# Two runs of packed 32x32 products in place of one, in a linear-attention kernel on one Trainium2 core

## The chip, the cores and the metric

The kernel runs on one core of a Trainium2 chip. The core has a matrix engine (TensorE, PE in the profile, with its weight loads shown apart as PEld), a vector engine (VectorE, DVE), a scalar engine (ScalarE, ACT), a general engine (GpSimd, POOL) and an engine that here only issues transfers (SyncE, SP). Matrix products go into PSUM, of which the kernel uses eight banks of 128 x 512 fp32 values; everything else lies in SBUF, and the inputs and the output in HBM. Each engine works off its own queue of instructions in order, and engines wait for each other by semaphores. The metric is the device time of one execution in microseconds; lower is better.

## The reference

Sixteen sequences of 256 tokens with 128 features go through twelve layers of attention without a softmax, then a layer norm, a gated feed-forward and a second layer norm. The core of a layer:

```python
for i in range(12):
    qkv = x @ Wqkv[i].T + bqkv[i]
    q, k, v = split(qkv)                # 16 heads of 8 features
    att = einsum('bhqd,bhkd->bhqk', q, k) * scale
    y   = einsum('bhqk,bhkd->bhqd', att, v)
    x   = y @ Wproj[i].T + bproj[i] + x
x = layernorm(x0 + x)
h = silu(x @ wg.T) * (x @ wu.T)
x = layernorm(x + h @ wd.T)
```

Without a softmax the order of the products is free: y = q (k^T v) per head, and k^T v is only 8 x 8 per head. The kernel goes further and never moves the tokens through the layers at all.

## The kernel before

Within a sequence a layer multiplies every token by one and the same matrix, which depends on the sequence, so the kernel carries one 128 x 128 matrix and one offset column per sequence (`tst`, 128 x 130 with two spare columns). Sixteen sequences are taken as eight *pairs* of two batches (`PB = 2`), and four pairs make a *set* (`G = 4`, `NO = 2`): two sets for each of the twelve layers, 24 in all. fp32 matrices that go through PE are split into a rounded high part and a low part (`thl`, `whl`, `yhl`), so that a product is three fast ones.

Per layer and pair, `products` (L420) makes K and V (`mm_kv`, L436 to L438, six full-size products of 256 columns), Q (`mm_q`, L444 to L446, three of 260 columns) and g0 times V (`mm_gv`, L457, two fp32 products of 128 columns, which the profile shows as four passes). Copies out of PSUM (L440, L449, L459) go through the helper `copy`, so the profile shows them at L205 (ACT) or L207 (DVE).

Per layer and set, `heads` (L480) does what is packed. `mm_m` (L493) makes the heads' small matrices in products of 128 rows by 32 columns (L501, and the offsets' L382 before them). DVE adds an offset (L511) and masks (L513), which gives `gm`: for each pair and batch a 128 x 32 strip that holds four 32 x 32 blocks. Then `mm_y` (L515) multiplies each 32 x 32 block of `gm` with the matching 32 rows of Q (130 columns) on PE's 32 x 32 tiles:

```python
for b in range(PB):
    for r, p in enumerate(pairs):
        for g in range(G):
            nc.tensor.matmul(bank(pys[r])[group(g + r), ...], gm[group(g), r * PB + b, :], qss[p][group(g), b, :], ...)
```

The loops over r and g address each of the 16 tiles once; the second batch addresses the same 16 again. A set has 2 x 4 x 4 = 32 such products in four PSUM banks (`pys`), and as each is fp32 it is issued as two passes with a weight load each: 64 rows at L519.

`projection` (L523) then casts y out of PSUM (L531, by ACT or DVE), takes the low part (L532, DVE), multiplies by the output weights (`mm_w`, L536 to L538; two more at L540 and L541 in the last layer), and adds to `tst` (L543). In the layers but the last, a cast by ACT (L545) and a subtraction by POOL (L546) make the next layer's `thl`. After the last layer each pair goes through the feed-forward (`ffn`, L575).

No instruction order is written out. Every step is an `Op` of a `Plan` with a cost per engine that may do it, what it reads and writes, and a priority. `Plan.run` (L118) is a list scheduler that runs when the program is built: it keeps a time for each engine, computes for each ready step when it could start, takes the earliest start and among those that could start by then the lowest priority, and emits it. The time at which a step may follow another is the other's end plus a constant: 300 for PE behind ACT, DVE or POOL, 30 for PE behind PE (L137). PSUM banks, raw weights and split weights are slots that the same planner hands out. Its costs only set the order and the choice of engine; on the chip semaphores decide. The step of y costs 1200 (L520), one product on rounded fp32 `0.447 n + 5`, that of `mm_m` 890 and 140 for each set of offsets that rides along.

In the built program the order on PE around a set is, in the layers from 2 on: three products of the last Q, twelve of K and V of the other set's first two pairs, the 64 rows of y, twelve of the other two pairs' K and V, one pair's L457, twelve of the projection, three pairs' L457, nine of Q, then the next set's `mm_m`.

Of the kernel before, what the change touches and what calls it, by code (L numbers as in the profile page):

```python
# [25 lines left out]
PB = 2  # L26
NP = B // PB
W = C + 2
# [8 lines left out]
G = 4  # L37
# [13 lines left out]
LSTEP = 0.05  # L51
WLEAD = 0.6
TAILW = 0.0001
AHEAD = 0.16
SPARE = 500

# [17 lines left out]
PE, ACT, DVE, POOL, SP = "pe", "act", "dve", "pool", "sp"  # L74
AFTER = {PE: 270, ACT: 160, DVE: 200, POOL: 180, SP: 3000}
TO_PE = 300


class Val:


    def __init__(self, kind=None):
        self.kind, self.slot = kind, None
        self.writers, self.readers, self.ops, self.left = [], [], [], 0


class Op:
    def __init__(self, n, costs, emit, prio):
        self.n, self.costs, self.emit, self.prio = n, costs, emit, prio
        self.end = self.engine = None  # L90
        self.deps, self.users, self.vals = set(), [], []


class Plan:
    def __init__(self, slots):
        self.slots, self.ops = slots, []

    def op(self, costs, emit, reads=(), writes=(), prio=0.0):

        o = Op(len(self.ops), costs, emit, prio)  # L100
        for v in reads:
            o.deps.update(v.writers)
        for v in writes:
            o.deps.update(v.writers, v.readers)
            v.writers, v.readers = [o], []
        for v in reads:
            if v not in writes:
                v.readers.append(o)
        o.vals = list(dict.fromkeys([*reads, *writes]))
        for v in o.vals:  # L110
            if v.kind:
                v.left += 1
                v.ops.append(o)
        for d in o.deps:
            d.users.append(o)
        self.ops.append(o)

    def run(self):  # L118
        free = dict.fromkeys(AFTER, 0.0)
        free.update({SP: 800.0, DVE: 4000.0, ACT: 3200.0, POOL: 4900.0})  # L120
        slots = {k: [(0.0, i) for i in range(n)] for k, n in self.slots.items()}
        left = {o: len(o.deps) for o in self.ops}
        for o in reversed(self.ops):
            o.tail = min(o.costs.values()) + 300 + max((u.tail for u in o.users), default=0)
        ready = [o for o in self.ops if not left[o]]
        takes = lambda o: [v for v in o.vals if v.kind and v.slot is None]
        while ready:
            found = []
            for o in ready:
                if any(not slots[v.kind] for v in takes(o)):  # L130
                    continue
                held = max((min(slots[v.kind])[0] for v in takes(o)), default=0.0)
                best, least = None, None
                for e, c in o.costs.items():
                    t = max(free[e], held)
                    for d in o.deps:
                        wait = TO_PE if e == PE and d.engine in (ACT, DVE, POOL) else 30 if d.engine == e == PE else AFTER[d.engine]  # L137
                        t = max(t, d.end + wait)
                    rank = t + c + (SPARE if e == DVE and o.prio > L - 1.6 else 0)
                    if best is None or rank < least:  # L140
                        best, least = (t, t + c, e), rank
                found.append((best, o))
            assert found, "no slot is free"
            first = min(b[0] for b, _ in found)
            (_, end, e), o = min(((b, o) for b, o in found if b[0] <= first), key=lambda x: (x[1].prio - TAILW * x[1].tail, -x[1].tail, x[1].n))
            o.engine, o.end = e, end
            free[e] = end
            ready.remove(o)
            for v in takes(o):
                s = min(slots[v.kind])  # L150
                slots[v.kind].remove(s)
                v.slot = s[1]
            o.emit(e)
            for v in o.vals:
                if v.kind:
                    v.left -= 1
                    if not v.left:
                        slots[v.kind].append((max(x.end for x in v.ops) + 200, v.slot))
            for u in o.users:
                left[u] -= 1  # L160
                if not left[u]:
                    ready.append(u)
        assert all(o.end is not None for o in self.ops)
        self.span = max(free.values())
# [14 lines left out]
def dve(n, fast=False):  # L179
    return 69 + n / (1.92 if fast else 0.96)  # L180


def pool(n):
    return 147 + 2.1 * n
# [7 lines left out]
def linear_attention_ffn_kernel(ctx: ExitStack, tc: tile.TileContext, x, xt, wall, wq0, bias, wg, wu, wd, out):  # L192
    nc = tc.nc
# [5 lines left out]
    plan = Plan({"bank": 8, "raw": RAW, "weights": WSLOTS, "turned": WSLOTS})  # L199
    banks = [ps.tile([128, 512], F32, name=f"bank{i}") for i in range(8)]  # L200
    bank = lambda v: banks[v.slot]
# [10 lines left out]
    def mul(e, dst, a, b):  # L212
        (nc.vector if e == DVE else nc.gpsimd).tensor_tensor(dst, a, b, ALU.mult)  # L213
# [55 lines left out]
    vq, vgv = [Val() for _ in range(NP)], [Val() for _ in range(NP)]  # L269
# [50 lines left out]
    qss = [t[:, : PB * W].rearrange("p (a b) -> p a b", b=W) for t in qgvs]  # L320
# [3 lines left out]
    vt, vc, vhi, vlo, vm, vg0, vkv, vyh, vyl, vqo, vw = (named() for _ in range(11))  # L324
# [48 lines left out]
    def offset_products(l, o):  # L373

        raw, pc = wts[l][0], Val("bank")
        c = tst[:, o * OB : (o + 1) * OB, C]

        def mm():
            for s in range(1 if l else 0, 3):
                for g in range(G):  # L380
                    cols = slice(32 * g, 32 * g + 32)
                    nc.tensor.matmul(bank(pc)[cols, s * OB : (s + 1) * OB], wraw[raw.slot][:, s * C : (s + 1) * C][:, cols], c, start=True, stop=True)  # L382
        return [raw, *vc[o * G : (o + 1) * G]], pc, mm
# [34 lines left out]
    vgm = sets()  # L418
# [55 lines left out]
    def first_offsets(o, prio):  # L474
        def fill(e):
            for p in range(o * G, (o + 1) * G):
                nc.gpsimd.tensor_copy(qss[p][:, :, C], qc[:, p * PB : (p + 1) * PB])
        plan.op({POOL: 600}, fill, [vqc[o]], vqo[o * G : (o + 1) * G], prio)

    def heads(l, o, prio, riders):  # L480

        raw = wts[l][0]
        pairs = range(o * G, (o + 1) * G)
        gm = gms[o]
        pm, pys = Val("bank"), [Val("bank") for _ in pairs]
        group = lambda g: slice(32 * (g % G), 32 * (g % G) + 32)
        src = [raw] if l == 0 else [vkv[p] for p in pairs]

        more = [(*r, *offset_products(*r)) for r in riders]

        def mm_m(e):  # L493
            for _, _, _, _, mm in more:
                mm()
            for p in pairs:
                for b in range(PB):
                    n = (p - o * G) * PB + b
                    tk = wraw[raw.slot][:, C : 2 * C] if l == 0 else kvs[p][:, b, 0, :]
                    for g in range(G):  # L500
                        nc.tensor.matmul(bank(pm)[group(g), n * 32 : n * 32 + 32], tk[:, group(g)], gvs[p][:, b, group(g)], start=True, stop=True)  # L501
        reads = [v for _, _, rs, _, _ in more for v in rs]
        if l == 0 and o == 1:

            reads += vw[:G]
        plan.op({PE: 890 + 140 * len(more)}, mm_m, [*(vgv[p] for p in pairs), *src, *reads], [pm, *(m[3] for m in more)], prio)
        for lo, oo, _, pc, _ in more:
            offsets(lo, oo, prio + (OFFSET if lo else 0), pc)
            if lo == 0:
                first_offsets(o, prio)  # L510
        plan.op({DVE: dve(OB * 32)}, lambda e: nc.vector.tensor_tensor(  # L511
            gm, bank(pm)[:, : OB * 32].rearrange("p (b j) -> p b j", j=32), kvo[:, o * OB : (o + 1) * OB], ALU.add), [pm, vkvo[o]], [vgm[o]], prio)
        plan.op({DVE: dve(OB * 32), POOL: pool(OB * 32)}, lambda e: mul(e, gm, gm, mask32.unsqueeze(1).to_broadcast([128, OB, 32])), [], [vgm[o]], prio)  # L513

        def mm_y(e):  # L515
            for b in range(PB):
                for r, p in enumerate(pairs):
                    for g in range(G):
                        nc.tensor.matmul(bank(pys[r])[group(g + r), b * W : (b + 1) * W], gm[group(g), r * PB + b, :], qss[p][group(g), b, :], start=True, stop=True)  # L519
        plan.op({PE: 1200}, mm_y, [vgm[o], *(vq[p] for p in pairs), *(vqo[p] for p in pairs)], pys, prio)  # L520
        return pys

    def projection(l, p, py, prio):  # L523
# [234 lines left out]
    for p in range(NP):  # L758
        ffn(p, L + FOFF + FSTEP * p - (AHEAD if p == NP - 1 else 0))
    plan.run()  # L760
# [31 lines left out]
```

## Time and profile before

| | |
|---|---|
| time, median of 3 runs | 306.25 us (306.08 to 306.49) |
| the profiled execution | 306.32 us, of which its span 304.6 us |
| instructions | 12894 |
| PE busy, products | 295.0 us, 5382 |
| PE rows at L519 (y, 32x32) | 1536, 25.8 us busy |
| PE rows at L501 (128x32) | 1536, 18.6 us busy |
| mean clock that TensorE was granted | 0.996 |

The profile is of one execution. Its span runs from the first to the last instruction; the device time has some 1.7 us around it. Products on PE are pipelined: a row's length is its latency, and rows overlap, so a start-to-start distance is what a product costs in a dense stream. In the page's slices each digit is the busy share of a fortieth of the span (7.6 us) in tenths. A line of the waits names the waiting group, what it waited for, the sum in us, how often, and the longest.

### The profile page before, as it was taken

How to read it: one execution, taken by the hardware profiler on the slowest of the kernel's cores; microseconds unless marked ns; L12 is line 12 of the kernel's file. 1: busy time of each engine (PE TensorE's matmuls, PEld its weight loads, DVE VectorE, ACT ScalarE, POOL GpSimd, SP SyncE). 2: the span in 40 equal slices, each digit the busy share in tenths (PEclk: the TensorE clock that was granted, in tenths of full speed). 3: DMA queues.
4: the chain of work that ended last, by engine and by line, in shares of the span. 5: the costliest groups of instructions: out<-in, count | busy, mean ns of one | idle time of the engine just before them, and what ended most of it. 6: DMA issues, size and time to landing. Idle time of an engine off the chain costs nothing.

```text
span 304.6 us, 12894 instructions
## 1 busy us (share of the span) xinstructions
PE 295.0 (97%) x5382; PEld 270.8 (89%) x5382; DVE 226.6 (74%) x685; ACT 221.2 (73%) x564; POOL 140.7 (46%) x232
## 2 busy tenths in 40 slices
PE   8999999999999999999999999999999999989981
PEld 8989999999999999999999999999999898868870
DVE  4796877777677676876768777786545689999993
ACT  3556877767777768777686666876887567888875
POOL 6246352334531445215442254324433458767783
PEclk9999999999999999999999999999999999999998
DMA  7634213112031120311302102130000000000224
GB/s 209 156 101 126 71 39 88 38 46 81 3 88 37 40 89 3 88 40 31 95 2 56 37 21 61 33 80 4 2 2 3 4 1 2 0 0 2 70 69 139
DMA packets 22490, 15.66 MB, mean 51 GB/s; under 512 B 1952, under 2 KB 19872, under 8 KB 22432
## 3 DMA queue, kind: packets, MB, share of 16 engines
q1 hardware_dynamic: 21872, 14.62, 17.2%
q8 instruction: 42, 0.69, 1.0%
q10 hardware_dynamic: 560, 0.22, 0.3%
q14 instruction: 16, 0.13, 0.1%
HBM read 8.02 MB, written 2.10 MB: 33 GB/s over the span
## 4 chain that ended last, share of the span: by engine, by line
PE 81%; DVE 11%; ACT 3%; issue 3%; POOL 0%; POOLq 0%; DVEq 0%
PE bank L457 14%; PE bank L436 8%; PE bank L519 8%; PE bank L438 7%; PE bank L437 7%; PE bank L501 5%; PE bank L444 5%; PE bank L538 4%; PE bank L537 4%; PE bank L536 4%; PE bank L445 3%; PE bank L446 3%; PE bank L338 3%; DVE st L599 2%; DVE xt L704 2%
## 5 line engine op out<-in xcount | busy, mean ns | idle before, releaser
L210 POOL TENSOR_TENSOR thl<-tst,thl 128x260 fp32r<-128x260 f32 x88 | 64.9, 769 | 123.2 <-ACT thl L205 123.2
L205 ACT COPY qgv<-bank 128x256 f32<-128x256 f32 x170 | 60.8, 377 | 20.7 <-PE bank L446 13.4
L205 ACT COPY kv<-bank 128x512 f32<-128x512 f32 (+1 forms) x93 | 53.4, 577 | 18.8 <-PE bank L438 13.6
L436 PE MATMUL bank<-whl,thl 128*128 128x256 f32 x176 | 51.8, 294 | 0.0
L438 PE MATMUL bank<-whl,thl 128*128 128x256 f32 x176 | 49.7, 282 | 0.0
L437 PE MATMUL bank<-whl,thl 128*128 128x256 f32 x176 | 49.4, 281 | 0.0
L457 PE MATMUL bank<-kv,g 128*128 128x128 f32 x352 | 46.0, 275 | 0.0
L543 DVE TENSOR_TENSOR tst<-bank,tst 128x260 f32<-128x260 f32 x96 | 36.9, 425 | 11.2 <-PE bank L538 9.0
L205 ACT CAST thl<-tst 128x260 fp32r<-128x260 f32 x88 | 33.1, 410 | 14.5 <-DVE tst L543 14.4
L457 PEld LDWEIGHTS bank<-kv,g 128*128 128x128 f32 x352 | 42.7, 191 | 0.4 <-issue 0.4
L450 DVE TENSOR_SCALAR qgv<-bank,bcol 128x2 f32<-128x2 f32 x88 | 19.3, 221 | 27.8 <-ACT qgv L205 23.4
L532 DVE TENSOR_TENSOR yhl<-bank,yhl 128x260 fp32r<-128x260 f32 x96 | 34.5, 421 | 3.0 <-ACT yhl L205 3.0
L436 PEld LDWEIGHTS bank<-whl,thl 128*128 128x128 f32 x176 | 33.1, 188 | 4.1 <-issue 3.8
L438 PEld LDWEIGHTS bank<-whl,thl 128*128 128x128 f32 x176 | 33.1, 188 | 0.2 <-POOL thl L210 0.2
L437 PEld LDWEIGHTS bank<-whl,thl 128*128 128x128 f32 x176 | 33.2, 189 | 0.0
L444 PE MATMUL bank<-thl,whl 128*128 128x260 f32 x88 | 28.9, 328 | 0.0
L519 PE MATMUL bank<-qgv,gm 32*32 32x130 f32 x1536 | 25.8, 280 | 0.2 <-DVE gm L213 0.2
L205 ACT CAST yhl<-bank 128x260 fp32r<-128x260 f32 (+1 forms) x62 | 22.4, 412 | 4.7 <-PE bank L519 4.5
L207 DVE CAST yhl<-bank 128x260 fp32r<-128x260 f32 x42 | 16.1, 424 | 12.9 <-PE bank L519 12.9
L445 PE MATMUL bank<-thl,whl 128*128 128x260 f32 x88 | 24.8, 282 | 0.0
L446 PE MATMUL bank<-thl,whl 128*128 128x260 f32 x88 | 24.7, 281 | 0.0
L519 PEld LDWEIGHTS bank<-qgv,gm 32*32 32x32 f32 x1536 | 17.2, 103 | 5.5 <-ACT kv L205 0.3
(155 smaller groups left out, 704.3 us busy)
## 6 DMA issues: line engine op xcount, KB each, us to landing
wraw<-wall SPq DMA_DIRECT2D x12, 256.0 KB, 2.9
wpt<-whl SPq DMA_DIRECT2D x24, 96.0 KB, 2.2
qgv<-x SPq DMA_DIRECT2D x8, 256.0 KB, 5.2
xt<-xt SPq DMA_DIRECT2D x8, 256.0 KB, 3.2
out<-kv SPq DMA_DIRECT2D x7, 256.0 KB, 2.3
wpt<-whl SPq DMA_DIRECT2D x24, 64.0 KB, 2.6
wpt<-whl SPq DMA_DIRECT2D x24, 32.0 KB, 1.9
wraw<-wg SPq DMA_DIRECT2D x1, 192.0 KB, 3.6
```

The costliest lines, as they stand in the source:

```text
L205: nc.scalar.copy(dst, src)
L210: (nc.vector if e == DVE else nc.gpsimd).tensor_tensor(dst, a, b, ALU.subtract)
L436: nc.tensor.matmul(o, hi[:, b, 0:C], hl(0, 1, 2), start=True, stop=False)
L437: nc.tensor.matmul(o, hi[:, b, 0:C], hl(1, 1, 2), start=False, stop=False)
L438: nc.tensor.matmul(o, lo[:, b, 0:C], hl(0, 1, 2), start=False, stop=True)
L444: nc.tensor.matmul(o, hl(0, 0), flat(hi), start=True, stop=False)
L445: nc.tensor.matmul(o, hl(0, 0), flat(lo), start=False, stop=False)
L446: nc.tensor.matmul(o, hl(1, 0), flat(hi), start=False, stop=True)
L457: nc.tensor.matmul(bank(pgv)[:, b * C : (b + 1) * C], g0[p][:, b, :], tv(b), start=True, stop=True)
L519: nc.tensor.matmul(bank(pys[r])[group(g + r), b * W : (b + 1) * W], gm[group(g), r * PB + b, :], qss[p][group(g), b, :], start=True, stop= ...
L532: plan.op({DVE: dve(PB * W)}, lambda e: nc.vector.tensor_tensor(yl, bank(py)[:, : PB * W], yh.bitcast(F32), ALU.subtract), [py, vyh[p]], [ ...
L543: plan.op({DVE: dve(PB * W)}, lambda e: nc.vector.tensor_tensor(ts, bank(pw)[:, : PB * W], ts, ALU.add), [pw], [vt[p], vc[p]], prio)
```

## The change

The step of y becomes two steps for each set, one per batch (`range(1)`, `range(1, PB)`), each with 16 products and a planner cost of 520. Both write the same four banks, so the planner runs the second behind the first, and the second's distance to the end of the first is now `APART = 300` in place of 30: a step of PE that can start within that time goes first. Readers of y depend on the second step alone. The first set of layer 0 keeps one step at cost 1200.

```diff
+APART = 300
 class Op:
-    def __init__(self, n, costs, emit, prio):
-        self.n, self.costs, self.emit, self.prio = n, costs, emit, prio
+    def __init__(self, n, costs, emit, prio, apart):
+        self.n, self.costs, self.emit, self.prio, self.apart = n, costs, emit, prio, apart
...
-    def op(self, costs, emit, reads=(), writes=(), prio=0.0):
-        o = Op(len(self.ops), costs, emit, prio)
+    def op(self, costs, emit, reads=(), writes=(), prio=0.0, apart=30):
+        o = Op(len(self.ops), costs, emit, prio, apart)
...
-                        wait = TO_PE if e == PE and d.engine in (ACT, DVE, POOL) else 30 if d.engine == e == PE else AFTER[d.engine]
+                        wait = TO_PE if e == PE and d.engine in (ACT, DVE, POOL) else o.apart if d.engine == e == PE else AFTER[d.engine]
...
-        def mm_y(e):
-            for b in range(PB):
-                for r, p in enumerate(pairs):
-                    for g in range(G):
-                        nc.tensor.matmul(bank(pys[r])[group(g + r), b * W : (b + 1) * W], gm[group(g), r * PB + b, :], qss[p][group(g), b, :], start=True, stop=True)
-        plan.op({PE: 1200}, mm_y, [vgm[o], *(vq[p] for p in pairs), *(vqo[p] for p in pairs)], pys, prio)
+        for run in ([range(1), range(1, PB)] if l + o else [range(PB)]):
+            def mm_y(e, run=run):
+                for b in run:
+                    for r, p in enumerate(pairs):
+                        for g in range(G):
+                            nc.tensor.matmul(bank(pys[r])[group(g + r), b * W : (b + 1) * W], gm[group(g), r * PB + b, :], qss[p][group(g), b, :], start=True, stop=True)
+            plan.op({PE: 520 if l + o else 1200}, mm_y, [vgm[o], *(vq[p] for p in pairs), *(vqo[p] for p in pairs)], pys, prio, APART if run[0] else 30)
```

Lines of the changed kernel are two higher than before from L100 on, and four higher behind `mm_y`.

## The prediction

> **What bounds the kernel now.** I read the page's head and its slices first, then what TensorE (PE) waited for, then the timeline of one layer, and last the final stretch.
>
> ```profile
> span 304.6 us, 12894 instructions
> PE 295.0 (97%) x5382; PEld 270.8 (89%) x5382; DVE 226.6 (74%) x685; ACT 221.2 (73%) x564; POOL 140.7 (46%) x232
> ...
> PE   8999999999999999999999999999999999989981
> ...
> DVE  4796877777677676876768777786545689999993
> ```
>
> PE is full in every slice up to the 35th; DVE only fills up in the last seven or so. A busy PE alone proves little, so the waits decide:
>
> ```profile
> PE bank L225 <- DVE qgv L223: 1.0, 1, 1.0
> PE bank L713 <- DVE xt L704: 1.0, 1, 1.0
> ...
> PE bank L519 <- DVE gm L213: 0.2, 1, 0.2
> ```
>
> Over the twelve layers PE waits for nobody but twice for 0.2 us (L519 and L538); the waits of a microsecond are at the start and in the feed-forward. So in the layers the time is the sum of PE's start-to-start distances, and whatever the change adds or saves there moves the end one for one. One run of y (L519) among its neighbours, PE alone:
>
> ```profile
> 151.64 0.28 PE L437 MATMUL bank<-whl,thl 128*128 128x256 f32 x1
> 151.76 0.28 PE L438 MATMUL bank<-whl,thl 128*128 128x256 f32 x1
> 151.97 1.07 PE L519 MATMUL bank<-qgv,gm 32*32 32x130 f32 x64
> 152.98 0.39 PE L436 MATMUL bank<-whl,thl 128*128 128x256 f32 x1
> 153.20 0.28 PE L437 MATMUL bank<-whl,thl 128*128 128x256 f32 x1
> 153.32 0.28 PE L438 MATMUL bank<-whl,thl 128*128 128x256 f32 x1
> ```
>
> First column: start. Full-size products follow each other every 0.118 us (151.64, 151.76; 153.20, 153.32). Into the run the step is 0.21, the run holds PE from 151.97 to 152.98, and the first full-size product behind it is followed only after 0.22. The 64 rows are 32 products, each issued as two passes. Cutting the timeline just before and just after the middle separates the two batches:
>
> ```profile
> 151.97 0.50 PE L519 MATMUL bank<-qgv,gm 32*32 32x130 f32 x32
> ...
> 152.29 0.75 PE L519 MATMUL bank<-qgv,gm 32*32 32x130 f32 x32
> ```
>
> The batches are unequal: 0.50 us for the first 32, 0.75 for the second, which begins 0.32 us into the run. The weight loads say why (PEld and its count, in three stretches of the same run):
>
> ```profile
> 151.90:152.22 0.32, 0.25 (x32) 0.24 (x33) 1.00 0.00 0
> 152.22:152.39 0.17, 0.17 (x33) 0.09 (x1) 1.00 0.00 0
> 152.39:152.79 0.40, 0.40 (x45) 0.37 (x31) 1.00 0.00 0
> ```
>
> Thirty-three loads go out at once, then one in 0.17 us, then 31: the second batch uses the same 16 tiles and cannot load until the first has let go of them. So one long run has a stall inside it as well as the switches at its ends.
>
> **The change, priced.** To the nanosecond, from the single records behind these rows (22 of the 24 runs have the same inner times): last full-size start to first y start 209; first y start to the start of the 32nd 235; to the 33rd 320, 34th 431, 64th 805; from the last y start to the next full-size start 199; from there to the one after 223. Without a run in between, two steps of 118 would stand in these places.
>
> (a) Removed: one run. It costs 209 + 805 + 199 + 223 - 236 = 1200 ns.
>
> (b) Added: two runs of 32. No trace shows such a run alone, but every piece has a row. Entry 209, 32 starts in 235, exit 199 + 223, less 236: 630 ns. Two are 1260, so a set loses 60 ns. Put the other way: the second batch costs 805 - 235 = 570 inside the long run, with its stall (235 to 431) and its slower pace (374 ns from the 34th to the 64th start); by itself it runs like the first, but pays 91 to enter (209 - 118), 199 to leave and 105 (223 - 118) for the first weights behind it: 630.
>
> Is the exit really 199 after a shorter run? The head's other packed products (L501, 128x32) say what it consists of:
>
> ```profile
> 159.06 0.75 PE L501 MATMUL bank<-qgv,kv 128*32 128x32 f32 x64
> 159.74 0.39 PE L444 MATMUL bank<-thl,whl 128*128 128x260 f32 x1
> 159.97 0.28 PE L445 MATMUL bank<-thl,whl 128*128 128x260 f32 x1
> ```
>
> There the last start to the next full-size start is 126 ns, and then 224 again. Their moving side is 32 columns, that of y 130; at the 111 ns per 128-column pass of L457 the difference is 85 ns, and 199 - 126 = 73. So the exit is the last product's streaming plus 86 to 98 ns (199 less 113, 126 less 28) that do not depend on what ran before. I take 199.
>
> Bounds. Low: if a short run leaves as L501 does (126), it costs 557, and a set gains 1200 - 1114 = 86 ns. High: the slowest first batch in the trace (the run at 26.5 us, second set of layer 0) takes 332 for its 32 starts; if every second run did, a set would lose 60 + 97 = 157 ns. The value taken is the plain one, +60, as 22 of the 24 first batches took 235.
>
> The pace inside a short run is the other thing to doubt. In the trace the first 16 starts take 100 ns, 6.7 each, and the second pass begins at 135. [...]
>
> (c) Number: 24 sets, the first of layer 0 excepted: 23 x 60 = 1.4 us. The order in which the changed program issues its instructions has 46 runs of half the length, and never two in a row: between them stand one pair's six K and V products (L436-438) from layer 2 on, two to six other full-size products in layers 0 and 1 and in the last set.
>
> (d) Moved. Around the run, before: q3 kv12 [y] kv12 gv2 w12 gv6; after: q3 kv12 [y] kv6 [y] kv6 gv4 w12 gv4 (w: the projection, L536-538; counts of instructions or products). The same products, and the same number of changes between fp32 and rounded fp32. Two waits come nearer. The casts of y (L531) start only when the second run is over, and w now has kv6 and gv4 ahead of it instead of kv12 and gv2. From the second run's first start: the next full-size start at 235 + 199 = 434, the sixth of kv 223 + 4 x 118 later at 1129, gv from 1247 with eight passes of 111 to 2024, w at some 2.05 us, and its third product, which needs the low part (L532), 324 ns behind at 2.38. On ACT the order is now the copy of the third pair's K and V (0.58) and then the cast of y (0.41): that copy can start when its products end, 0.07 us after the second run's start, so the cast ends at 1.1 and L532 on DVE (0.42) at 1.55. About 0.8 us to spare; cost nothing, cover named. Without the cover each 0.1 us late would cost 2.2 us over the sets. The wait for gm is as before, since M, q3 and kv12 stand in the same order before the first run. The DMA queue's order is unchanged; POOL's changes only in small copies and offsets and in the feed-forward.
>
> (e) The tail. From 254 us DVE sets the pace:
>
> ```profile
> 254.00:270.00 16.00, 14.98 (x87) 12.29 (x86) 15.79 (x30) 11.96 (x24) 11.86 (x10) 1.00 0.00 1
> 270.00:290.00 20.00, 20.00 (x99) 16.37 (x98) 19.37 (x40) 18.34 (x39) 15.49 (x16) 1.00 0.10 27
> ```
>
> (third bracketed column DVE: 35.2 of 36 us; fourth ACT: 30.3). The planner deals the tail's work out anew: three scalings L622 leave DVE and become twelve L627 on ACT; two casts to hh, one subtraction and one copy to yhl go the other way. With the rows' median lengths, DVE's work behind the last mask product falls from 67.9 to 67.3 us, ACT's behind the last cast to thl rises from 72.1 to 74.5. If DVE binds throughout, -0.5; if ACT takes over, up to +2.4. ACT has 5.7 us of idle in that stretch, and the chain runs through both, so I take 0 and keep -0.5 to +2.4.
>
> Sum: the profiled execution took 306.32 us, span 304.6 and 1.7 around it; 306.32 + 1.4 = 307.7. It lies 0.07 above the median of 306.25, so for the median 307.6.
>
> **Rivals.** *Short runs are cheap (faster).* One mechanism: the stall between the batches (200 ns) goes, and the exit shrinks as the array empties sooner. It decides from 587 ns a run downwards (2 x 587 = 1200 less 27, and 23 x 27 = 0.6 us). For it: the second batch is plainly the dearer one in the trace. Against: L501's exit splits as shown. At 557 a run: 306.3 - 2.0 = 304.3.
>
> *Given back in the tail (no change).* PE's lateness meets a tail that DVE bounds: 1.4 - 0.5 and some of DVE's idle time before 254: 306.6. Against: DVE's tail cannot start before the last set's y.
>
> *A new wait at the projection (slower still).* ACT's K and V copy, now ahead of the casts, delays y by more than the 0.8 us: 0.1 us a set gives 307.6 + 2.2 = 309.8.
>
> *The split does not happen:* excluded by the built order.
>
> **Numbers.** Forecast 0.50; cheap short runs 0.24; tail 0.13; new wait 0.13. Measurements of this kernel spread by 0.13%, so 0.2% (0.6 us) is about what tells from no change. Faster: 0.25 (the second case and a little of the tail's); slower: 0.61 (forecast with its tail mostly, and the new wait); same: 0.14. Range 304.2 to 309.9, from the low bound of the run to its high bound; the forecast's own, with the tail, 307.0 to 309.0.
>
> **What would show it.** The changed profile should have 46 rows of x32 with full-size products between, each 434 ns from first start to the next full-size start, and a layer's two sets about 0.12 us longer than the 19.5 of before; no new PE wait in the layers; the last set's y about 1.3 us later, and the way from there to the end as long as before. I am wrong if the next full-size start comes under 390 ns after a short run's first, if PE waits for DVE at the projection, or if the tail shifts by over 1 us.

## The result and the profile after

The changed kernel takes 307.61 us (median of 5 runs, 307.30 to 308.47), the kernel before 306.49 us in the same session (5 runs). The ratio is 1.0043, 95% interval 1.0027 to 1.0058: slower by 1.3 us by the ratio and 1.1 by the medians. The head of its page:

```profile
span 305.8 us, 12852 instructions
...
PE 296.4 (97%) x5382; PEld 266.2 (87%) x5382; DVE 224.2 (73%) x683; ACT 221.9 (73%) x576; POOL 139.3 (46%) x231
...
PE   8999999999999999999999999999999999999981
```

As many products as before, PE full as before, 1.2 us more span. One set in PE's timeline (start, length, line, count):

```profile
152.75 0.50 PE L523 MATMUL bank<-qgv,gm 32*32 32x130 f32 x32
153.19 0.39 PE L438 MATMUL bank<-whl,thl 128*128 128x256 f32 x1
153.41 0.28 PE L439 MATMUL bank<-whl,thl 128*128 128x256 f32 x1
...
153.88 0.28 PE L440 MATMUL bank<-whl,thl 128*128 128x256 f32 x1
154.09 0.50 PE L523 MATMUL bank<-qgv,gm 32*32 32x130 f32 x32
154.53 0.38 PE L438 MATMUL bank<-whl,thl 128*128 128x256 f32 x1
154.75 0.28 PE L439 MATMUL bank<-whl,thl 128*128 128x256 f32 x1
```

Each run now looks like the first batch of the long run: 0.50 us long, the next full-size start 0.44 behind its first (153.19 - 152.75), the one after 0.22 later, and 0.21 to enter again (153.88 to 154.09). In the single records 43 of the 46 runs have exactly 235 ns from first to last start, and the way out is 199 or 200 ns in all of them. PE's waits:

```profile
PE bank L227 <- DVE qgv L225: 1.0, 1, 1.0
PE bank L721 <- DVE xt L708: 0.8, 1, 0.8
...
PE bank L542 <- DVE yhl L536: 0.2, 1, 0.2
PE bank L523 <- DVE gm L215: 0.2, 1, 0.2
```

The view names nothing new: the projection (L542) and the first run of y (L523) wait 0.2 us once, as before. By the single starts two first runs of y are late, by 0.15 us in the second layer (the one at 46.85 us) and by 0.26 at 201.96 us; before, one is, by 0.24 at 200.92 us. The tail, by its stretches (DVE is the third bracketed column, ACT the fourth):

```profile
254.00:270.00 16.00, 15.56 (x93) 12.78 (x91) 15.42 (x31) 13.44 (x32) 9.45 (x9) 1.00 0.01 2
270.00:290.00 20.00, 20.00 (x99) 16.17 (x98) 19.79 (x41) 17.69 (x39) 15.65 (x16) 1.00 0.10 27
```

DVE has 35.2 of 36 us, as before; ACT 31.1 in place of 30.3.

Where the 1.2 us of span went, from the starts of y's runs and of the last product, counted from PE's first product: the first set starts 0.24 us sooner (17.20 against 17.44); from the first set to the last it takes 1.51 more (225.20 against 223.70); from there to the last product 0.43 less (55.74 against 56.17); and behind that 0.38 more. In the steady layers the distance from set to set is 9.79 us in place of 9.73 and 9.75 in turn: over the 16 sets from the seventh on 156.89 against 156.06, which is 52 ns a set.

### The profile page after: what moved, and what is told of

The parts are those of the page before. It is cut to its first block, busy times and chain, and to the rows that moved or that the text cites. A ratio compares the mean times of both kernels' runs of the same rounds, so it can differ in the third digit from the quotient of the medians.

```text
span 305.8 us, 12852 instructions
## 1 busy us (share of the span) xinstructions
PE 296.4 (97%) x5382; PEld 266.2 (87%) x5382; DVE 224.2 (73%) x683; ACT 221.9 (73%) x576; POOL 139.3 (46%) x231
## 4 chain that ended last, share of the span: by engine, by line
PE 83%; DVE 11%; ACT 3%; issue 2%; POOLq 0%; DVEq 0%; POOL 0%
PE bank L459 14%; PE bank L438 9%; PE bank L523 7%; PE bank L440 6%; PE bank L439 6%; PE bank L503 5%; PE bank L446 5%; PE bank L542 4%; PE bank L541 4%; PE bank L540 4%; PE bank L447 3%; PE bank L448 3%; PE bank L340 3%; PE bank L384 2%; PE bank L675 2%; DVE xt L708 2%
## 5 line engine op out<-in xcount | busy, mean ns | idle before, releaser
L207 ACT COPY qgv<-bank 128x256 f32<-128x256 f32 x173 | 62.8, 378 | 19.9 <-PE bank L448 11.0
L438 PE MATMUL bank<-whl,thl 128*128 128x256 f32 x176 | 53.7, 305 | 0.0
L440 PE MATMUL bank<-whl,thl 128*128 128x256 f32 x176 | 49.6, 282 | 0.0
L439 PE MATMUL bank<-whl,thl 128*128 128x256 f32 x176 | 49.5, 281 | 0.0
L459 PE MATMUL bank<-kv,g 128*128 128x128 f32 x352 | 46.8, 276 | 0.0
L209 DVE CAST yhl<-bank 128x260 fp32r<-128x260 f32 (+1 forms) x42 | 16.4, 431 | 28.3 <-PE bank L523 28.3
L523 PE MATMUL bank<-qgv,gm 32*32 32x130 f32 x1536 | 24.4, 281 | 0.3 <-DVE gm L215 0.2
L619 POOL TENSOR_TENSOR rs<-ve,mhalf 128x4 f32<-128x4 f32 x16 | 16.9, 1056 | 8.1 <-DVE ve L606 5.4
```

The costliest lines, as they stand in the source:

```text
L207: nc.scalar.copy(dst, src)
L438: nc.tensor.matmul(o, hi[:, b, 0:C], hl(0, 1, 2), start=True, stop=False)
L439: nc.tensor.matmul(o, hi[:, b, 0:C], hl(1, 1, 2), start=False, stop=False)
L440: nc.tensor.matmul(o, lo[:, b, 0:C], hl(0, 1, 2), start=False, stop=True)
L459: nc.tensor.matmul(bank(pgv)[:, b * C : (b + 1) * C], g0[p][:, b, :], tv(b), start=True, stop=True)
```

## The experiments

Three questions: is it the split or the new order around it; is it a fixed price for each run; and what makes the second half of a long run slow. Medians first:

| kernel | runs of y a set | median us | distance of sets, steady | late entries into y, sum us |
|---|---|---|---|---|
| before | 1 | 306.0 to 306.7 | 9.73, 9.75 | 0.24 |
| after | 2 | 307.61 | 9.79 | 0.41 |
| order alone | 1 | 307.45 | 9.72, and 9.85 where gm is late | 1.21 |
| order alone, POOL in pieces | 1 | 307.25 | 9.73, and 9.86 where gm is late | 0.54 |
| after, POOL in pieces | 2 | 307.54 | 9.79 | 0.00 |
| old order, split | 2 | 308.96 | 9.77, 9.79 | 0.75 |
| POOL tied elsewhere | 1 | 311.21 | 9.71, and 10.32 where gm is late | 4.80 |
| POOL tied elsewhere | 2 | 309.80 | 9.77 to 9.79, and 10.08 where gm is late | 2.47 |

Each kernel was timed beside the kernel before, and the ratios below are to that. The last two columns come from the profiled run of each. An entry is late by what the step from the last full-size start to the first of y exceeds 209 ns, counted where it exceeds 220.

**The order alone.** The changed kernel's plan, but the first of the two steps issues all 32 products and the second none:

```diff
-                for b in run:
+                for b in range(PB) if not run[0] else ():
```

> The changed kernel's order and its plan on every engine, but the first of the two steps issues all 32 products of y and the second none. Theory (the second entry and exit cost 60 ns a set more than the stall they replace, and nothing else moved): 23 x 60 = 1.4 us come back, 307.6 - 1.4 = 306.2, and the run is again 805 ns from first to last start. Rival (the new order around y, or the re-dealt tail, costs the time): stays at 307.3 to 307.9.

Measured: 307.45 us (10 runs, 306.70 to 308.36), ratio to before 1.0038 (1.0023 to 1.0053). By the median the rival wins: the 1.4 us did not come back. The profiled execution is one of the fastest of the ten (306.74 us): from its first run of y to its end it is 0.8 us longer than the kernel before, and the changed kernel 1.5. The trace shows why. PE before a run that is late:

```profile
142.02 0.28 PE L439 MATMUL bank<-whl,thl 128*128 128x256 f32 x1
142.14 0.28 PE L440 MATMUL bank<-whl,thl 128*128 128x256 f32 x1
142.47 1.06 PE L523 MATMUL bank<-qgv,gm 32*32 32x130 f32 x64
```

0.33 us into the run in place of 0.21. It waits for gm, and gm for DVE's mask product (L215); the same kernel's DVE, and then its POOL:

```profile
141.45 0.22 DVE L452 TENSOR_SCALAR qgv<-bank,bcol 128x2 f32<-128x2 f32 x1 [0.41 <-ACT qgv L207]
141.59 0.73 DVE L215 TENSOR_TENSOR gm<-gm,mask 128x256 f32<-128x256 f32 x1
...
140.75 1.29 POOL L212 TENSOR_TENSOR whl<-wraw,whl 128x512 fp32r<-128x512 f32 x1
```

The mask product takes 0.73 us where it usually takes 0.42, and POOL's subtraction for the split weights is running until 142.04, 0.45 us into it. In the changed kernel the two only just touch, and the product is stretched to 0.48, which nobody waits for:

```profile
142.19 0.48 DVE L215 TENSOR_TENSOR gm<-gm,mask 128x256 f32<-128x256 f32 x1
...
141.09 1.30 POOL L212 TENSOR_TENSOR whl<-wraw,whl 128x512 fp32r<-128x512 f32 x1
```

In the kernel before POOL starts 1.57 us ahead of the mask product and has finished:

```profile
141.47 0.42 DVE L213 TENSOR_TENSOR gm<-gm,mask 128x256 f32<-128x256 f32 x1
...
139.90 1.29 POOL L210 TENSOR_TENSOR whl<-wraw,whl 128x512 fp32r<-128x512 f32 x1
```

So the run isn't an undoing of the split alone: without it the new order has a wait of its own. Sets without that wait stand 9.72 us apart, as in the kernel before. In the 11th and 12th layers, where neither kernel has a late entry, three sets in a row start 9.73 us apart here (210.85, 220.58, 230.31) and 9.79 in the changed kernel (211.74, 221.53, 231.32).

**The old order with the split.** The kernel before with its own plan; the second batch is issued behind PE's next step. DVE, ACT, POOL and SP keep their instructions and their order:

```diff
+            batch(0)
+            if l + o:
+                plan.late = lambda: batch(1)
...
+            late, self.late = self.late, None
             o.emit(e)
+            if late and e == PE:
+                late()
```

> The kernel before with its own plan; only the place of the second batch differs: it is issued behind PE's next step (six K and V products from layer 2 on). DVE, ACT, POOL and SP get the same instructions in the same order as before. Theory (the split itself costs 60 ns in 23 sets): 306.3 + 1.4 = 307.7, ratio about 1.0045, no new PE wait. Rival (the re-planned order and tail cost the time, the split is free): 306.3, ratio 1.000.

Measured: 308.96 us (6 runs, 308.36 to 309.33), ratio 1.0090 (1.0068 to 1.0112). The split is not free, but this is twice what was expected. PE's waits name part of the rest:

```profile
PE bank L548 <- DVE yhl L542: 1.1, 1, 1.1
...
PE bank L524 <- DVE gm L218: 0.3, 1, 0.3
```

The 1.1 us is in layer 0, whose first set isn't split: there DVE sat 0.58 us until the second layer's weights had landed, and cast y afterwards:

```profile
19.18 0.97 DVE L212 CAST whl<-wraw 128x512 fp32r<-128x512 f32 x1 [0.58 <-DMA wraw<-wall]
20.07 0.75 DVE L212 CAST yhl<-bank 128x260 fp32r<-128x260 f32 x2
```

Why they landed later in this program isn't settled. It is 0.9 us more than the step there takes in the kernel before; with the late entries (0.75 against 0.24) that makes 1.4 of the 2.8 us and leaves 1.4. One run that entered late, at 183.40 us, also took 433 ns from first to last start in place of 235, which is 0.2 of it. In the steady layers the sets stand 9.77 and 9.79 apart against 9.73 and 9.75: 40 ns each.

**Four runs.** The changed kernel with runs of 8 products on 8 tiles:

```diff
-        for run in ([range(1), range(1, PB)] if l + o else [range(PB)]):
+        for n, run in enumerate([(b, rs) for b in range(PB) for rs in (range(2), range(2, G))] if l + o else [None]):
```

> The changed kernel with four runs a set (8 products on 8 tiles each) in place of two. Theory (each run pays a fixed 91 + 199 + 105 = 395 ns, and inside it 135 ns to the second pass and 47 for eight steps): 577 ns a run, a set 4 x 577 - 1260 = 1.05 us dearer, 307.6 + 24 = 331 to 332 us if nothing else waits. Rival (a switch is cheap once the array holds little, and the price goes with the products): a run at half of 630, 307.6 to 310.

Measured: 333.45 us (4 runs), ratio 1.0883 (1.0858 to 1.0908).

```profile
115.23 0.28 PE L440 MATMUL bank<-whl,thl 128*128 128x256 f32 x1
115.44 0.45 PE L523 MATMUL bank<-qgv,gm 32*32 32x130 f32 x16
115.83 0.39 PE L438 MATMUL bank<-whl,thl 128*128 128x256 f32 x1
116.05 0.28 PE L439 MATMUL bank<-whl,thl 128*128 128x256 f32 x1
```

In 0.21, then 0.39 to the next full-size start, then 0.22: 0.21 + 0.39 + 0.22 less two steps of 0.118 is 0.58 us for half the work of a run that costs 0.63. The price is nearly all the run's own. 25.8 us over the changed kernel against 24 worked out.

**One product between.** The old order with the split, but mostly one full-size product between the runs:

```diff
                     nc.tensor.matmul(o, hi[:, b, 0:C], hl(0, 1, 2), start=True, stop=False)
+                    if plan.held:
+                        plan.held()
+                        plan.held = None
```

> As the old order with the split, but only one full-size product stands between the two runs in most sets. Theory A (a run of 32 passes is quick whenever its tiles are free): the second run again has 235 ns from first to last start, a set costs 209 + 235 + 199 + 209 + 235 + 199 + 223 less 3 x 118 = 1155 ns, 45 under one run: 306.3 - 1.0 = 305.3. Theory B (the quick pace lasts as long as what was queued ahead, and so short a gap doesn't refill the queue): the second run takes 300 to 450 ns, the time is 306.8 to 310.

Measured: 307.95 us (one run).

```profile
113.62 0.50 PE L530 MATMUL bank<-qgv,gm 32*32 32x130 f32 x32
114.06 0.39 PE L444 MATMUL bank<-whl,thl 128*128 128x256 f32 x1
114.37 0.50 PE L530 MATMUL bank<-qgv,gm 32*32 32x130 f32 x32
114.81 0.39 PE L448 MATMUL bank<-whl,thl 128*128 128x256 f32 x1
```

Neither expectation held. The time lies in B's range, but by chance: the second run is as quick as the first (235 to 237 ns), so B is wrong. The 105 ns that A hoped to save are paid all the same: from the one product between to the run behind it are 0.31 us, 0.21 plus those 105. The late start behind a run belongs to the first full-size product itself (its row is 0.39 long, not 0.28), and more of them between two runs don't hide it. The sets are 9.79 apart, as with six between.

**The loops turned, one run.** The kernel before with pairs outside and batches inside, and then with both batches directly on the same tile:

```diff
-            for b in range(PB):
-                for r, p in enumerate(pairs):
+            for r, p in enumerate(pairs):
+                for b in range(PB):
                     for g in range(G):
```

> The kernel before with one run, its loops turned: pairs outside, batches inside, so that a tile gets its second product 4 products after its first, not 16. Theory A (the stall inside a long run is a tile that must let go of its first product before it can load the next): a hold comes at each of the four pairs, the run grows from 805 ns to 1200 or more, the program gets slower by 9 us or more. Theory B (the stall comes after 32 passes because that many were queued ahead, whichever tiles they use): the run stays at 805 and the time at 306.3.

> As the run with pairs outside, but the two batches follow each other directly on the same tile. Theory A: every second product waits for the one just ahead, so 16 holds; the run takes 16 x some 200 to 330 ns, 3 us or more, and the program some 50 us longer. Theory B: unchanged, 306.3.

Measured: 313.88 us (4 runs), ratio 1.0244 (1.0223 to 1.0265), and 316.36 us (one run). With pairs outside:

```profile
115.83 1.42 PE L519 MATMUL bank<-qgv,gm 32*32 32x130 f32 x64
117.17 0.38 PE L436 MATMUL bank<-whl,thl 128*128 128x256 f32 x1
117.40 0.28 PE L437 MATMUL bank<-whl,thl 128*128 128x256 f32 x1
```

The run holds PE for 1.34 us in place of 1.01: coming back to a tile soon costs something, so B's "unchanged" is wrong. But A is wrong too. In the single records a tile's second product starts 110 ns behind the second pass of its first (passes at 0, 135, 245, 360), with no hold, and all three loop orders have starts at 320 and 431 ns (within 1 ns), where the first 32 passes are out. With pairs outside, the 33rd pass by the loops is the first on a tile that the run has not used yet, and it too starts only at 321.

**The runs cut by pairs.** The changed kernel, 32 passes a run as there, but on 8 tiles that each get both batches:

```diff
-                for b in run:
-                    for r, p in enumerate(pairs):
+                for b in range(PB):
+                    for r, p in list(enumerate(pairs))[(2 if run[0] else 0) : (4 if run[-1] else 2)]:
```

> The changed kernel with its two runs cut by pairs in place of batches: 8 tiles, each with both batches, 32 passes a run. Theory A (the hold in the long run comes from coming back to a tile): the 17th pass waits some 200 ns, as the 33rd does in the long run. Theory N (the hold comes with the 33rd pass of a run, whichever tiles): no hold; second passes from 135, the second batch from 245 and 380, the last start at about 427 ns, so a run is 190 ns dearer than with 16 tiles, 46 runs 8.8 us: about 316.

Measured: 315.5 us (one run).

```profile
117.18 0.28 PE L440 MATMUL bank<-whl,thl 128*128 128x256 f32 x1
117.39 0.68 PE L523 MATMUL bank<-qgv,gm 32*32 32x130 f32 x32
117.99 0.38 PE L438 MATMUL bank<-whl,thl 128*128 128x256 f32 x1
```

0.60 us to the next full-size start, against 0.44; the records have the 17th pass at 246 and the last start at 407. No hold at the 17th pass: N. Coming back to a tile costs 110 ns behind its last pass, and the hold of 200 ns with the slower pace behind it is seen behind the first 32 passes of the runs of 64 on 32x32 tiles, and in no run of 32 or 16 that entered on time (with the old order one of 32 that entered late took 433 ns).

**POOL's subtraction tied elsewhere.** The plan with one run, and with two, where that subtraction follows the mask product of the set before:

```diff
-        after = [vlo[G - 1]] if l > 1 else []
+        after = [vgm[1]] if l > 1 else []
```

> One run a set on the changed plan, as in the run with the order alone, but POOL's subtraction for the split weights is tied to another step, so that it leaves the stretch in which DVE masks gm. If the late gm (DVE's mask product stretched from 0.42 to 0.73 us while POOL works) is why that run did not get its 1.4 us back: the mask product is at 0.42 again, no entry over 215 ns, 306.2. If not: 307.4.

> The partner of the run before it: the same plan with the two runs. The split by itself: 1.4 us above its partner, so 307.6. Rival (the split is free): the same as its partner.

Measured: 311.21 us (5 runs, ratio 1.0165, 1.0143 to 1.0187) and 309.80 us (6 runs, 1.0118, 1.0095 to 1.0141). Both expectations failed: POOL got a further small step ahead of the subtraction and came later, so gm was later still (4.80 and 2.47 us of late entries), and the kernel with two runs is the faster of the pair: there 0.59 us of the subtraction is left when the mask product starts, with one run 0.87.

**POOL's subtraction in pieces.** The order alone, and the changed kernel, with the 512 columns in four instructions of 128:

```diff
-        plan.op({POOL: pool(n)}, lambda e: sub(e, whl[hl.slot][:, 1, a:], ...
+        plan.op({POOL: pool(n)}, lambda e: [sub(e, whl[hl.slot][:, 1, i : i + C], ... for i in range(a, 4 * C, C)], ...
```

> The changed kernel's order with one run a set, as in the run with the order alone, and POOL's subtraction for the split weights (128x512, 1.29 us) issued in four pieces of 128 columns. Theory (a DVE instruction on two SBUF operands stands still while a POOL instruction runs, so the mask product was stretched by what was left of the long one): the product takes at most 0.55 us, the late entries of up to 0.16 us into every second run shrink to under 0.03, and the 1.4 us of the split come back: about 306.3. Rival (gm is late for another reason, or the stretch goes by POOL's work and not by its instruction): as the order alone, 307.4.

> The partner: the changed kernel with two runs, POOL's subtraction in four pieces. The split by itself, with gm on time in both: 50 ns in 23 sets by the steady distance of the sets seen so far, so 1.0 to 1.4 us above its partner, 307.3 to 307.7. Rival (the split is free): as its partner.

Measured: 307.25 us (12 runs, ratio 1.0020, 1.0010 to 1.0031) and 307.54 us (12 runs, 1.0026, 1.0011 to 1.0040). With two runs the late entries are gone; with one they are halved, and the stretch of the mask product is not. With one run, DVE and POOL:

```profile
141.37 0.76 DVE L215 TENSOR_TENSOR gm<-gm,mask 128x256 f32<-128x256 f32 x1
...
140.53 1.90 POOL L212 TENSOR_TENSOR whl<-wraw,whl 128x128 fp32r<-128x128 f32 x4
```

A piece takes 0.47 us, not a quarter of 1.29. By the records the third piece starts 3 ns behind the product, which ends 0.76 us later, 0.28 after that piece; the fourth piece is then 0.65 long. So the product waits for one instruction of POOL's and no longer for all four, but one is long enough. As an undoing of the split the pair is still not clean: 0.3 us apart, intervals overlapping. By the profiled executions, from the first set's y to the last's the kernel with two runs takes 0.57 us more (224.50 against 223.94), though the other has 0.54 us of late entries: together 1.1, or 48 ns in each of 23 sets. From the last set's y to the end it takes 0.20 less (62.39 against 62.59), and its first set starts 0.27 sooner. Sets that enter on time show the split alone: with one run they follow each other after 9.734 and 9.746 us in turn, as in the kernel before, so the new order by itself costs them nothing; with two runs it is 9.794 and 9.786, 50 ns more.

## Why the prediction was right, and where it was not

**The price of a run (b): right.** 209 to enter, 235 inside, 199 and 223 out were read off the long run and off L501, and 43 of 46 runs have those inner 235 ns. "So a set loses 60 ns": 52 in the steady layers of the changed kernel, 40 with the old order, where nothing but the split differs. Summed by kind of step over eight steady sets, the runs with the K and V products around them cost 66 ns a set more than before (57 with the old order), and the steps of the projection, with the old order also those of Q, take 16 ns less. So the term was sized well, and those 16 ns were left out; no run shows why they are saved.

**The low bound: out.** L501's short exit (126 ns) is seen behind no run of y: even runs of 16 passes leave in 199. The rival with cheap short runs falls with it, and four runs a set show the fixed part directly.

**Why the long run's second half is slow: wrong.** The prediction said that the second batch "uses the same 16 tiles and cannot load until the first has let go of them". Turned loops and the runs cut by pairs show a tile taking its second product after 110 ns without a hold; the hold comes behind the 32nd pass, whatever tiles are used. Why PE holds there stays open. The sum used only the measured starts, so it stood.

**The number of sets (c): right.** 46 short runs and one long one.

**The moved waits (d): half right.** The projection has its cover: in the steady layers its third product starts 2.38 to 2.39 us behind the second run's first start (2.38 worked out), 0.70 to 0.95 us after the low part of y is ready (0.8 worked out). But "The wait for gm is as before" is the step that failed. The order on PE ahead of the first run is the same, and the prediction looked no further; yet POOL's weight subtraction moved from ending before DVE's mask product to overlapping it, every second set. In the code it follows the low part of the set's last pair, which hangs on the projection, and the projection now starts 3.40 us behind y's first start in place of 2.88; the subtraction comes 0.5 us later against that start too (7.91 against 7.41). In the changed kernel the overlap is short and hidden. With one run on that order it is a wait: 1.21 us of late entries, 0.84 of them in the steady layers.

**The tail (e): near.** Taken as 0; from the last set's y to the last product it is 0.43 us shorter, and 0.38 longer behind it. The way from that y to the end is thus as long as before (62.35 us against 62.40), and that y starts 1.27 us later, as forecast.

The total of 307.6 was thus met by its main term, with small ones that cancel, and that they cancel is luck: -0.24 at the start (which lies anywhere from 16.95 to 17.97 us in the runs with one or two runs of y), 1.51 through the layers (1.32 expected for 22 sets; 0.17 of it are late entries), -0.43 and +0.38 at the end. What is not shown is that undoing the split on the new order wins back 1.3 us. It wins 0.2 to 0.3 by the medians: the new order then waits for gm, and the tail is 0.2 us longer. Set by set it is shown: the split costs 40 to 60 ns a set in every pair whose sets aren't late; whether the program sees that depends on what else is due at the same moment.

## What to carry to other kernels

Count the switches between full-size products and products on small tiles, and price one from start-to-start distances: here about 395 ns for a short run (91 in, 199 out, 105 behind it), besides its products. Cutting a run pays only when the part cut off costs more than that inside the long run; here it was 570 against 630. When you undo one part to prove a cause, look at the waits again: on a schedule this tight another wait can stand just behind the one you took away.

## What the runs showed of the hardware

In the kernel before, 22 of the 24 runs of 32x32 products start their first 16 products 6.7 ns apart and the second passes of these at the same pace (235 ns to the 32nd start), then stand for about 200 ns with one start at 320, and go on with a product every 16.6 ns (805 ns in all; twice 235 if cut). The products on 128x32 tiles show no such break in the steady layers: L382 and L501 start their 80 passes within 706 ns, 8 to 9 ns each from first to last, and no two starts are over 33 ns apart.

DVE's mask product, whose two operands both lie in SBUF, was longer in sets where a POOL instruction ran at its start (with the pieces, one that began 3 ns behind it): it was 0.73 us long with 0.45 us of POOL's left at its start, 0.48 with 0.20 left, 0.76 with a piece of 0.47, and 0.42 by itself. In each case the excess over 0.42 is the remainder less 0.13 or 0.14. Where POOL's subtraction started second, 0.13 us behind the mask product (at 64.06 us in the changed kernel), the mask product took 0.42 and the subtraction 1.42, where the next six take 1.28 to 1.30. DVE's product ahead of the mask, of which one operand comes out of a bank (L513 there), took 0.41 to 0.43 us in all 24 sets, also where 1.3 us of POOL's subtraction were left at its start. In pieces, the subtraction lengthened the mask product by what one piece had left, not by what all of them had.
